# Near mirrored blocks of layer 0's first convolution through HBM, and a new order of work

## The chip, the cores and the metric

The kernel runs on one core of a Trainium2 chip. A core has a matrix engine (TensorE, PE in the profile, with its weight loads listed apart as PEld), a vector engine (VectorE, DVE), a scalar engine (ScalarE, ACT), a general engine (GpSimd, POOL) and a sync engine (SyncE, SP) that here only issues DMAs. Matmuls read SBUF and write PSUM, which has eight banks of 512 float32 columns. The metric is the device time of the whole program in microseconds: the median of 3 runs before is 2375.07 us (2373.53 to 2380.12).

## What is computed

Sixteen graphs (B = 16) of 1,024 nodes with 128 features each, in float32, go through four graph layers, each behind a layer norm and a ReLU and added to its input. All layers use the same dense 1024 x 1024 adjacency `adj` of the graph. Only layer 0 is touched by the change in what it computes where:

```python
def _adapt_conv(h, edge_weight, W, b, is_last):
    h = h @ W + b
    norm = jnp.linalg.norm(h, axis=-1, keepdims=True)
    nh = h / jnp.maximum(norm, EPS)
    cos = jnp.einsum('bij,bkj->bik', nh, nh)
    ew = edge_weight * cos
    h = jnp.einsum('bpq,bqc->bpc', ew, h)
    if not is_last:
        h = jax.nn.relu(h)
    return h
```

Layer 0 applies this three times in a row, with `edge_weight = adj`. The product `cos` (1024 x 1024) is symmetric. Layer 1 sums over neighbours and applies two linear maps, layer 2 is an attention with tanh scores, and layer 3 is an attention whose scores `e + e^T` are symmetric as well.

## The kernel before, in words

**Blocks.** A graph is cut into 8 x 8 blocks of 128 nodes. A row of blocks of the square matrix (`cos` or the scores) is made in two halves of four blocks (`HALVES`), each in one PSUM bank. So row j, half s is one bank of 128 x 512.

**The class `Square`** (from line 1387) makes such a symmetric matrix with half of the multiplications. In `row(j, s)` TensorE multiplies only the blocks on and above the diagonal (line 1415). Blocks below it are mirrored copies of blocks made before. For the near ones, those whose row and column lie in the same half, `keep` lets ACT copy the blocks to the right of the diagonal from PSUM to the SBUF tile `near` (line 1450), and `row` lets TensorE turn them (a transpose through the identity matrix) into the bank of the later row (line 1425). There are six near blocks in each half: one turn for row 1, two for row 2, three for row 3, and the same for rows 5, 6 and 7 in the second half.

The far blocks, with row in 0 to 3 and column in 4 to 7, go another way in graphs 1 to 13, where `far` holds: VectorE transposes each 32 x 32 square of them in place on its way from PSUM to the tile `quart` (line 1437), and `send` writes this to a buffer in HBM (line 1459) and fetches it with four DMAs (line 1469) so that every square stands where it belongs in the tile `got`. Rows 4 to 7 then read their first half from `got` in SBUF.

**What reads a row.** In `layer0`, one VectorE instruction per row and half (line 1645) multiplies the bank (or `got`) with the row's `1/norm` and the adjacency, `ew = cos * rn * adjT`, over 512 columns. Then `accumulate` (line 1478, convolutions 0 and 1) or `accumulate_nodes` (line 1489, convolution 2) multiplies `ew` with `h` on TensorE and adds over the rows j = 0 to 7, in that order, in two PSUM banks `acc`. ACT evicts each bank through a ReLU to `hT`, the input of the next convolution. Convolution 0 gets its own operand `hTn` by HBM also (`squares`, lines 1189 to 1202).

**The order.** The kernel first makes a list of operations, each with an engine, a length, and the buffers that it reads and writes. `Plan.order` then picks, one after the other, the operation with the smallest due time whose inputs are issued and whose buffers have a free slot. A due time is the graph's number times `PERIOD` (144.24) plus an entry of the table `TIMES`, which has one number per kind of operation; other entries hold for the first and last two graphs. `KINDS` says how many buffers of each kind may be in use at once, and how many by graphs younger than the oldest unfinished one. The result is a fixed order of instructions on every engine and on SP's queue. Up to three graphs are in work at a time, so that TensorE does one graph's sums while another waits for VectorE or for memory.

Three lines by which an operation gets its place:

```python
due = TIMES[o.key + o.edge if o.key + o.edge in TIMES else o.key][o.nth]
o.rank = (o.batch * PERIOD + due, o.seq)
...
o = next((o for o in sorted(ready, key=lambda o: (o.rank, o.seq)) if fits(o)), None)
```

Of the kernel before, what the change touches and what calls it, by code (L numbers as in the profile page):

```python
# [12 lines left out]
ALU = mybir.AluOpType  # L13
AX = mybir.AxisListType

P = 128
N = 1024
NB = N // P
D = 128
# [195 lines left out]
def tile_adj_preln(  # L215
# [40 lines left out]
    FLAGS = set("CabcdkxhyzTGmrHWMD3n")  # L256
# [62 lines left out]
    for load_it in first:  # L319
# [13 lines left out]
        "adjT": ("big", 17, 16), "adjL": ("big", 14, 4), "x": ("big", 7, 3), "w4": ("big", 21, 24),  # L333
        "chunk": ("big", 9, 8), "near": ("near", 2, 1), "quart": ("big", 5, 8), "got": ("got", 1, 1),
        "ps": ("bank", 8, 6), "acc": ("bank", 7, 6), "small": ("small", 13, 26), "row": ("row", 3, 2),
        "hbm": ("hbm", 3, 2), "hrow": ("hrow", 1, 1), "mask": ("mask", 5, 5), "dot": ("dot", 8, 5),
# [4 lines left out]
        "T DMA raw <0": [-19.5, -30.5, -48.25, -41.6, -61.6, -75.05, -5.6, -8.8],  # L341
        "T PE raw <0": [-17.1, -16.8, -16.3, -16.25, -14.25, -15.95, -19.95, -10.65, -19.15, -14.9, -15.05,
            -34.8, -5.6, 13.9, -0.2, 26.3],
        "T ACT adjT <0": [-54.3, -17.2, -22.5, -25.2, -23.65, -17.05, -24.1, -19.25, -8.5, -3.25, 4.25, 4.65,
            7.05, 1.25, -5.95, 27],
        "T DVE su <0": [50.4],
        "x DMA x <0": [-19.55, -75.2],
        "0 DVE st <0": [-46.85, -22.65],
        "0 DVE mv <0": [-18.35],
        "0 POOL rstd <0": [-31.25],  # L350
        "0 DVE nb <0": [-31.8],
        "0 DVE hn <0": [-31.8],
        "0 ACT hn <0": [-53.5],
        "0 PE ps <0": [-17.05, -17.9],
        "0 ACT hT <0": [-58.3, -37.9],
        "00 PE psP <0": [-16.35, -46.85],
        "00 DVE h <0": [-30.8, -18.25],
        "00 PE ps <0": [-33.85, -20.2],
        "00 ACT hTn <0": [-18.95, -21.35],
        "00 ACT sq <0": [-19, -23.4],  # L360
        "00 DVE ss <0": [-16.75, -16.8, -15.5],
        "00 POOL rn <0": [-24.55],
        "00 PE sq <0": [-19.9, -12.6, -12.45, -23.35, -13.9, -17.15, -8.6, -23.65, -6.3, -5.4, -38.1, 3.85,
            -34.5, -17.15, 15.35, 2.15, -3.3, -5.6, 22.9, 15.35, 1.1, 29.25],
        "00 ACT near <0": [-23.6, -53.35, -7.5, -3.35, 2.15, 24.6],
        "00 DVE ew <0": [-41.35, -7.5, -29.95, -20.25, -14.55, -0.65, 3.15, 0.8, -0.5, 1.6, 7.15, 1.05, 0.25,
            18.4, 17.3, 1.05],
        "00 ACT quart <0": [-39.85, -19.2, -39.85, -3.6],
        "00 PE acc0 <0": [-6.35, -3.35, 17, 1.55, -1.85, 3.85, -4.1, 13.8, 18.1, 1.4, 20.4, 26.75, 21.8,
            32.5, 14.05, 24.35],  # L370
        "00 POOL params <0": [-0.75, 4.8, 1.4, 36.45, 20.4, 18.95, 14.6],
        "00 DMA params <0": [-27.4],
        "00 DVE params <0": [35.2, 37.7, 35.2, 70.35, 70.35],
        "00 PE params <0": [37.2, 38.35, 72.05],
        "00 ACT hT <0": [24.55, 43.65],
        "01 PE psP <0": [-1.55, -9.25],
        "01 DVE h <0": [42.8, 43.4],
        "01 PE ps <0": [44.3, 45.8],
        "01 ACT hTn <0": [41.8, 46.55],
        "01 ACT sq <0": [41.15, 38.65],  # L380
        "01 DVE ss <0": [48.2, 39.8, 40.2],
        "01 POOL rn <0": [53.15],
        "01 PE sq <0": [34.45, 47.75, 46.1, 57, 52.35, 40.35, 52.25, 50.05, 54.5, 49.75, 41.9, 57.15, 57.2,
            64.65, 65.45, 54.45, 64.9, 60.05, 68.45, 52.85, 66.35, 69.95],
        "01 ACT near <0": [35.25, 59.5, 43.5, 58.85, 59.1, 70.95],
        "01 DVE ew <0": [48.6, 66.5, 53.65, 57.7, 55.3, 52, 54.9, 68.65, 59.8, 61.85, 64.3, 68.9, 59.95,
            62.75, 61, 70.2],
        "01 ACT quart <0": [57.15, 51.8, 54.55, 57.4],
        "01 PE acc0 <0": [58.35, 37, 54.6, 70.2, 59.45, 65.6, 61.85, 60.35, 53.2, 50.4, 66.45, 72, 67.9,
            71.05, 50.3, 71.5],  # L390
        "01 ACT hT <0": [70.5, 73.15],
        "02 PE psP <0": [52.25, 74.2],
        "02 DVE h <0": [72.55, 70.5],
        "02 PE ps <0": [71.8, 77.3],
        "02 ACT hTn <0": [73.95, 80.25],
        "02 ACT sq <0": [76.7, 65.9],
        "02 DVE ss <0": [70.8, 78.05, 79.3],
        "02 POOL rn <0": [87],
        "02 PE sq <0": [80.2, 82.35, 81.65, 87.15, 80.95, 84.05, 85.05, 84.5, 84.55, 88.8, 86.4, 91.3, 91.8,
            66.75, 84.9, 96.75, 97.3, 85.75, 97.75, 100.9, 89.3, 100.3],  # L400
        "02 ACT near <0": [72.1, 93.55, 83.8, 82.75, 71.8, 89.3],
        "02 DVE ew <0": [82.1, 82.95, 84, 78.95, 95.8, 90.3, 96.05, 79.35, 95.45, 100.65, 95.8, 101.2, 75.7,
            93.05, 78.9, 91.5],
        "02 ACT quart <0": [81.4, 83.35, 87.15, 91.85],
        "02 PE acc0 <0": [82.65, 91.55, 87.95, 91.5, 91.25, 93.75, 100.15, 84.35, 100.2, 101.85, 102.45,
            105.25, 100.65, 103.05, 94.15, 106.85],
        "02 DVE x <0": [89.85, 114.75],
        "T DMA adjT <1": [-129.75, -221.3, -169.05, -212.7, -210.4, -169.1, -204.2, -217.15],
        "T DVE adjT <1": [-141.7, -138.05, -140.15, -129.95, -122, -117.65, -114.8, -114.6],
        "T ACT su <1": [-139.85, -107.05, -109.9, -104.85, -100.25, -112.55, -110.1, -95.2],  # L410
        "1 DVE st <0": [111.95, 111.5],
        "1 DVE mv <0": [93.85],
        "1 POOL rstd <0": [107.65],
        "1 DVE nb <0": [113.9],
        "1 DVE hn <0": [109.1],
        "1 ACT hn <0": [125.3, 117.65],
        "1 DVE x <0": [136.7, 134.95, 139.35],
        "1 DMA adjL <0": [59.95, 59.15, -24.85, 49.85, 132.5, 134.85, 93.65, 118.95],
        "1 DVE adjL <0": [101.65, 57, 134.6, 108.15, 119, 123.05, 130.95, 129],
        "1 PE acc1 <0": [114, 110.25, 123.5, 127.2, 124.8, 134.45, 122.45, 123.85, 123.7, 124.75, 127.6,  # L420
            126.65, 127.45, 131.6, 129.15, 127.8],
        "1 ACT g <0": [126.8, 128.05],
        "1 PE py <0": [131.8, 131.75, 131.75, 132.05],
        "1 ACT y1 <0": [132.55, 131.6, 137.7, 134.1],
        "1 PE py2 <0": [132.3, 132.15],
        "2 DVE st <0": [139.4, 128.85],
        "2 DVE mv <0": [118.75],
        "2 POOL rstd <0": [138.9],
        "2 DVE nb <0": [142.45],
        "2 DVE hn <0": [142.4],  # L430
        "2 ACT hn <0": [132.9, 129.85],
        "2 PE ps <0": [144.25, 144.15],
        "2 ACT hnT <0": [124.6, 93.2],
        "2 DVE alone <0": [138.85],
        "2 DVE x <0": [156.9, 185.75, 183.1],
        "2 PE psP <0": [148.65, 144.15, 144.2],
        "2 ACT h <0": [142.95, 139.4, 153.85],
        "2 DVE hrow <0": [149.7],
        "2 PE pf <0": [155.7],
        "2 ACT hfl <0": [159.45],  # L440
        "2 PE pt <0": [155.75],
        "2 ACT sr <0": [148.4],
        "2 DMA sd <0": [159.85],
        "2 DMA s1 <0": [158.25],
        "2 DVE h <0": [156.95],
        "2 ACT e2 <0": [144.55, 145.45, 145.3, 155.55, 143.05, 167.15, 163.25, 167.2, 167.25, 167.9, 164.45,
            167.9, 173.55, 175.1, 167.95, 166.3],
        "2 DVE e2 <0": [162.25, 163.05, 164.8, 164.75, 86.05, 81.75, 77.9, 77.85, 172.25, 165.85, 167.4,
            166.25, 158.75, 158.65, 172.65, 178.9],
        "2 PE acc2 <0": [158.05, 166.7, 147.55, 165.8, 163.25, 150.1, 172.65, 168.45, 164.6, 157.9, 168.9,  # L450
            170.85, 141.9, 167.65, 160.85, 177.65, 175.4, 171.65, 175.2, 177.5, 175.5, 172.1, 170.25, 149.5],
        "2 DVE rden <0": [185.75, 134.75, 134.1, 183.15],
        "3 DVE st <0": [186.45, 168.3],
        "3 DVE mv <0": [184.4],
        "3 POOL rstd <0": [186.7],
        "3 DVE nb <0": [168.2],
        "3 DVE hn <0": [171.55],
        "3 ACT hn <0": [183.55, 252.45],
        "3 PE ps <0": [197.3, 190.45, 194.1, 157.05],
        "3 ACT hnT <0": [183.65, 182.3],  # L460
        "3 PE pg <0": [197.3, 196.2],
        "3 ACT gT <0": [192.7, 203],
# [1118 lines left out]
    def layer0(b, xt, aT, prepared):  # L1581
# [8 lines left out]
        for i in range(3):  # L1590
# [46 lines left out]
            for j in range(NB):  # L1637
                ew = chunk(f"ew_{k}_{j}")
                for s, (lo, hi) in enumerate(HALVES):
                    pc, view = square.row(j, s)  # L1640
                    if "k" in FLAGS:
                        square.keep(j, s, pc)
# [556 lines left out]
```

## Time and profile before

The profiled execution took 2375.19 us, of which 2373.4 are the span from the first to the last instruction.

| | us | share of the span |
|---|---|---|
| TensorE busy | 2343.0 | 99% |
| VectorE busy | 2036.7 | 86% |
| ScalarE busy | 1445.6 | 61% |
| GpSimd busy | 253.4 | 11% |
| 16 DMA engines, queue 1 | | 59.8% |

The groups around the change, with how often they occur, their busy time and the mean of one:

| line | what | count | busy us | mean ns |
|---|---|---|---|---|
| 1425 | TensorE turns, sq from near | 768 | 147.0 | 273 |
| 1425 | TensorE turns, sq from quart | 192 | 28.0 | 273 |
| 1450 | ACT copies, near from sq, three shapes | 384 | 140.0 | 367 |
| 1437 | VectorE transposes, quart from sq, 512 columns | 208 | 143.5 | 699 |
| 1645 | VectorE products, ew from sq, 512 columns | 612 | 432.4 | 738 |
| 1645 | VectorE products, ew from got, 512 columns | 156 | 112.9 | 752 |

The busy time of a group counts overlapping instructions once; the mean is the length of one instruction from start to end. Instructions of an engine overlap in part, so that the distance from start to start, which is what an engine really spends on one, is read from the timeline and not from the mean. The granted TensorE clock was 0.997 over the span.

### The profile page before, as it was taken

What the parts mean: (1) busy time and instruction counts of PE and PEld (TensorE: products, weight loads), DVE (VectorE), ACT (ScalarE), POOL (GpSimd) and SP (SyncE); (2) the same over time, 40 slices, a digit from 0 to 9 for tenths busy, and PEclk for the clock granted to TensorE, in tenths of its full rate; (3) what the DMA queues carried; (4) which work ended last, traced back from release to release, by engine and by line L of the source; (5) the groups of instructions that cost most, each with busy time, mean ns of one, the idle gap of its engine ahead of it and who ended that gap; (6) DMA issues with size and microseconds to landing.
All of it is one profiled execution on the core that took longest, in us unless ns stands there. A gap on an engine that the chain in (4) does not pass through costs nothing.

```text
span 2373.4 us, 35020 instructions
## 1 busy us (share of the span) xinstructions
PE 2343.0 (99%) x11577; PEld 1551.8 (65%) x11577; DVE 2036.7 (86%) x5570; ACT 1445.6 (61%) x2561; POOL 253.4 (11%) x168
## 2 busy tenths in 40 slices
PE   8999999999999999999999999999999999999997
PEld 5568566675757657576675766757566575765764
DVE  6658899998989989898998989989899898887777
ACT  5416764747567565666656667565666657656375
POOL 3000010101101100010101101101010100100012
PEclk9999999999999999999999999999999999999999
DMA  9135649486594957939587594856949577272200
GB/s 198 60 106 116 125 116 191 121 159 143 146 175 134 185 107 164 183 98 198 117 164 153 135 185 127 170 122 164 176 115 188 115 155 146 63 123 64 72 1 18
DMA packets 997253, 314.30 MB, mean 132 GB/s; under 512 B 682456, under 2 KB 978528, under 8 KB 997072
## 3 DMA queue, kind: packets, MB, share of 16 engines
q1 hardware_dynamic: 976912, 301.35, 59.8%
q10 hardware_dynamic: 19264, 9.70, 1.4%
q8 instruction: 92, 1.51, 0.3%
q0 software_dynamic: 896, 1.01, 0.2%
q14 instruction: 89, 0.73, 0.1%
HBM read 227.50 MB, written 84.47 MB: 131 GB/s over the span
## 4 chain that ended last, share of the span: by engine, by line
PE 95%; DVE 3%; DMA 1%; ACT 1%; SPq 0%; issue 0%; POOL 0%; ACTq 0%; DVEq 0%
PE acc L1478 36%; PE sq L1415 20%; PE acc L1489 19%; PE psP L1249 6%; PE sq L1425 4%; PE py L1713 2%; PE py L1259 2%; PE ps_hTn L1178 1%; PE pg L1259 1%; PE psN L1249 1%; DVE e L1957 1%; DVE e L1916 1%; PE ps_hnT L1178 1%; PE ps_h3T L1178 1%; DMA x<-in_x_dram 1%; DVE e L1825 0%
## 5 line engine op out<-in xcount | busy, mean ns | idle before, releaser
L1645 DVE SCALAR_TENSOR_TENSOR ew<-sq,rn,adjT 128x512 f32<-128x512 f32 x612 | 432.4, 738 | 69.8 <-PE sq L1425 40.7
L1478 PE MATMUL acc<-ew,h 128*128 128x512 f32 x1024 | 476.6, 593 | 0.3 <-DVE ew L1645 0.3
L1415 PE MATMUL sq<-hTn 128*128 128x512 f32 (+3 forms) x1152 | 430.2, 487 | 0.4 <-ACT hTn L1271 0.4
L1450 ACT COPY near<-sq 128x128 f32<-128x128 f32 (+2 forms) x384 | 140.0, 367 | 325.5 <-PE sq L1425 256.3
L1478 PEld LDWEIGHTS acc<-ew,h 128*128 128x128 f32 x1024 | 181.5, 190 | 164.8 <-issue 134.5
L1415 PEld LDWEIGHTS sq<-hTn 128*128 128x128 f32 x1152 | 193.9, 191 | 129.9 <-issue 92.5
L1489 PEld LDWEIGHTS acc<-h,ew 128*128 128x128 f32 x2048 | 244.6, 192 | 33.4 <-issue 30.1
L1489 PEld LDWEIGHTS acc<-h,e 128*128 128x128 f32 x2048 | 236.6, 192 | 21.9 <-issue 16.8
L1489 PE MATMUL acc<-h,ew 128*128 128x128 f32 x2048 | 250.3, 275 | 0.0
L1478 PE MATMUL acc<-e,hs 128*128 128x512 f32 x512 | 240.4, 597 | 2.8 <-DVE top L1937 1.5
L1489 PE MATMUL acc<-h,e 128*128 128x129 f32 x2048 | 238.1, 275 | 0.8 <-DVE e L1825 0.8
L1478 PE MATMUL acc<-adjL,hn 128*128 128x512 f32 x512 | 231.9, 596 | 2.0 <-DVE adjL L1696 2.0
L1171 POOL TENSOR_TENSOR rstd<-ve,mhalf 128x8 f32<-128x8 f32 x64 | 105.2, 1644 | 787.3 <-DVE ve L1330 769.9
L1916 DVE CUSTOM_DVE_ANT_0 e<-mask,sq 128x512 f32<-128x512 int8 x204 | 136.1, 680 | 48.3 <-ACT near L1450 46.3
L1825 DVE SCALAR_TENSOR_TENSOR e<-adjT,e 128x512 f32<-128x512 f32 x256 | 162.7, 684 | 12.4 <-ACT e L1821 12.0
L1948 ACT ACTIVATE e<-e,top 128x1024 f32<-128x1024 f32 x128 | 146.6, 1146 | 41.4 <-DVE top L1937 40.0
L1957 DVE TENSOR_TENSOR e<-e,adjT 128x512 f32<-128x512 f32 x248 | 169.1, 701 | 2.5 <-ACT e L1948 2.5
L1171 POOL TENSOR_TENSOR rn<-ss,mhalf 128x8 f32<-128x8 f32 x48 | 83.3, 1736 | 817.3 <-DVE ss L1632 700.1
L1478 PEld LDWEIGHTS acc<-adjL,hn 128*128 128x128 f32 x512 | 95.6, 191 | 112.2 <-issue 102.6
L1425 PEld LDWEIGHTS sq<-ident,near 128*128 128x128 f32 x768 | 101.4, 141 | 81.8 <-issue 56.0
L1478 PEld LDWEIGHTS acc<-e,hs 128*128 128x128 f32 x512 | 91.4, 192 | 95.2 <-issue 72.5
L1817 ACT ACTIVATE e<-s,h 128x1024 f32<-128x1024 f32 x128 | 143.8, 1139 | 13.4 <-DMA s<-sd 13.4
(167 smaller groups left out, 3782.0 us busy)
## 6 DMA issues: line engine op xcount, KB each, us to landing
adjL<-in_adj_dram SPq DMA_DIRECT2D x128, 512.0 KB
adjT<-in_adj_dram SPq DMA_DIRECT2D x480, 128.0 KB
by_hbm<-quart SPq DMA_DIRECT2D x104, 512.0 KB
got<-by_hbm SPq DMA_DIRECT2D x416, 128.0 KB
s<-sd SPq DMA_DIRECT2D x15, 512.0 KB
out_dram<-z ACTq DMA_DIRECT2D x15, 512.0 KB
d_hT<-hn SPq DMA_DIRECT2D x14, 512.0 KB
hT<-d_hT SPq DMA_DIRECT2D x56, 128.0 KB
```

Of the source, the lines that this page charges most:

```text
L1171: pool_op(1.64, [src], [dst], lambda: nc.gpsimd.tensor_tensor(dst.t, src.t, mhalf, op=ALU.pow))
L1249: nc.tensor.matmul(dst.t[:, (c - lo) * n : (c - lo + 1) * n], one(srcT, c), w, start=True, stop=True)
L1415: lambda: nc.tensor.matmul(dst.t[:, (first - lo) * P :], one(leftT, j), some(rightT, first, hi), start=True, stop=True),
L1425: nc.tensor.transpose(cols(dst.t, r), cols(kept.t, p), ident)
L1478: lambda s=s, lo=lo, hi=hi: nc.tensor.matmul(acc[s].t, cols(h.t, at, w), span(ew.t, lo, hi), start=(j == 0), stop=(j == NB - 1)),
L1489: nc.tensor.matmul(a.t[:, (c - lo) * n : (c - lo + 1) * n], cols(ew.t, c), h.t[:, at * w : at * w + n], start=(j == 0 and c == lo), stop=( ...
L1645: lambda view=view, ew=ew, rn=rn, j=j, lo=lo, hi=hi: nc.vector.scalar_tensor_tensor(like(view(), span(ew.t, lo, hi)), view(), rn.t[:, j : ...
L1817: lambda e=e, j=j: nc.scalar.activation(e.t[:, 0:N], s1.t[:, 0:N], AF.Tanh, bias=h.t[:, j * E2 + D + 1 : j * E2 + D + 2]),
L1825: lambda e=e, j=j, lo=lo, hi=hi: nc.vector.scalar_tensor_tensor(span(e.t, lo, hi), span(aT[j].t, lo, hi), 0.0, span(e.t, lo, hi), op0=ALU. ...
L1916: lambda e=e, view=view, mask=mask, peak=peak, s=s, lo=lo, hi=hi: nc.vector.tensor_tensor_reduce(like(view(), span(e.t, lo, hi)), like(vie ...
L1948: lambda e=e, top=top, tot=tot: nc.scalar.activation(e.t[:, 0:N], e.t[:, 0:N], AF.Exp, bias=top.t, accum_out=tot.t),
L1957: lambda e=e, j=j, lo=lo, hi=hi: nc.vector.tensor_mul(span(e.t, lo, hi), span(e.t, lo, hi), span(aT[j].t, lo, hi)),
```

## The change

A second flag in the class `Square`, `near_too`, is set for convolution 0 of layer 0 in graphs 2 to 13 (`far(b, 0)` and `b > 1`; of the letters "ABV" only "A" is among the flags; for layer 3 the letter "X" is absent). There, the near blocks are mirrored like the far ones: VectorE transposes their 32 x 32 squares from PSUM to one of two tiles `laid`, a store puts them in HBM, and four fetches per half bring them to a tile `back`. TensorE turns none of them, and ACT copies none. The rows that have mirrored near blocks are read in two pieces, one from PSUM and one from `back`. All entries of `TIMES` are new, and so are most of `KINDS`.

```diff
-    FLAGS = set("CabcdkxhyzTGmrHWMD3n")
+    FLAGS = set("CabcdkxhyzTGmrHWMD3nA")
...
-        "adjT": ("big", 17, 16), "adjL": ("big", 14, 4), "x": ("big", 7, 3), "w4": ("big", 21, 24),
-        "chunk": ("big", 9, 8), "near": ("near", 2, 1), "quart": ("big", 5, 8), "got": ("got", 1, 1),
-        "ps": ("bank", 8, 6), "acc": ("bank", 7, 6), "small": ("small", 13, 26), "row": ("row", 3, 2),
-        "hbm": ("hbm", 3, 2), "hrow": ("hrow", 1, 1), "mask": ("mask", 5, 5), "dot": ("dot", 8, 5),
+        "adjT": ("big", 16, 16), "adjL": ("big", 13, 5), "x": ("big", 5, 3), "w4": ("big", 23, 33),
+        "chunk": ("big", 11, 11), "near": ("near", 2, 1), "quart": ("big", 6, 6), "back": ("big", 7, 1),
+        "got": ("got", 1, 1), "ps": ("bank", 8, 8), "acc": ("bank", 7, 4), "small": ("small", 28, 22),
+        "row": ("row", 4, 5), "hbm": ("hbm", 2, 3), "hrow": ("hrow", 2, 2), "mask": ("mask", 5, 5),
+        "dot": ("dot", 7, 7),
...
+        "00 DMA near": [-46.5, -23.3],
+        "00 DMA back": [-64.45, -19.05],
...
-        "00 ACT hT": [-37.35, -17.2],
+        "00 ACT hT": [-24.35, -11.7],
...
+            if near_too:
+                self.laid = [Buf("near", [P, 6 * P], f"laid_{k}_{s}") for s in range(2)]
+                self.back = [Buf("back", [P, N], f"back_{k}_{s}") for s in range(2)]
+            else:
+                self.near = Buf("near", [P, 6 * P], f"near_{k}")
...
+            if self.near_too and lo < j < hi:
+                back, (c, x, y) = self.back[s], self.MIRRORED[n]
+
+                def shares():
+                    return back.t[:, 0 : 6 * P].rearrange("p (x c i) -> p c x i", c=2, i=SQ)[:, c, x:y]
+
+                return [(dst, lambda: by_block(dst.t[:, n * P :], D, 4 - n), j, hi), (back, shares, lo, j)]
...
+        MIRRORED = {1: (0, 8, 12), 2: (0, 0, 8), 3: (1, 0, 12)}
+        LAID = {0: ((1, 1, 2, 0), (2, 2, 0, 0)), 1: ((2, 2, 1, 0),), 2: ((3, 1, 2, 1),)}
...
+            if self.near_too and lo <= j and first < hi:
+                laid = self.laid[s]
+                for q, n, x, c in self.LAID[j - lo]:
+                    dve(
+                        V(n * P) + 0.04, [blk(read, q, q + n)], [(laid, (j - lo) * P, (j - lo + 1) * P)],
+                        lambda q=q, n=n, x=x, c=c: nc.vector.transpose(
+                            laid.t.rearrange("p (h x c i) -> p h x c i", x=3, c=2, i=SQ)[:, :, x, c : c + n],
+                            read.t[:, q * P : (q + n) * P].rearrange("p (q h i) -> p h q i", h=P // SQ, i=SQ),
+                        ),
+                    )
+                if j - lo == 2:
+                    self.send_near(s)
+                return
...
+        def pieces(self, j, s):
+
+            if (j, s) not in self.known:
+                for j2 in range(j, j + QUARTER) if self.near_too else (j,):
+                    for s2 in (0, 1) if self.near_too else (s,):
+                        self.known[j2, s2] = self.row(j2, s2)
+                        self.keep(j2, s2, self.known[j2, s2][0][0])
+            return self.known.pop((j, s))
+
+        def send_near(self, s):
+
+            laid, back = self.laid[s], self.back[s]
+            by_hbm = Buf("hbm", [N, D], f"near_hbm_{self.k}_{s}")
+
+            def rows():
+                return by_hbm.t[0 : 6 * P].rearrange("a f -> (a f)")
+
+            op(
+                "DMA", 0.7, [laid], [by_hbm],
+                lambda: nc.sync.dma_start(
+                    rows().rearrange("(h p e) -> p h e", p=P, e=6 * SQ),
+                    laid.t.rearrange("p (h e) -> p h e", e=6 * SQ),
+                ),
+                lat=2.2,
+            )
+
+            def squares_to_places():
+                src = rows().rearrange("(h g a x e) -> h a x g e", h=P // SQ, g=P // SQ, a=SQ, e=2 * SQ)
+                for h in range(P // SQ):
+                    nc.sync.dma_start(
+                        back.t[h * SQ : (h + 1) * SQ, 0 : 6 * P].rearrange("p (x g e) -> p x g e", g=P // SQ, e=2 * SQ), src[h]
+                    )
+
+            op("DMA", 1.5, [by_hbm], [back], squares_to_places, lat=2.4)
...
-            square = Square(k, hTn, hTn, "abc"[i] in FLAGS and far(b, i))
+            square = Square(k, hTn, hTn, "abc"[i] in FLAGS and far(b, i), "ABV"[i] in FLAGS and far(b, i) and b > 1)
...
-                    pc, view = square.row(j, s)
-                    if "k" in FLAGS:
-                        square.keep(j, s, pc)
-                    o = dve(
-                        V(HALF, True), [pc, rn, blk(aT[j], lo, hi)], [blk(ew, lo, hi)],
...
+                    pieces = square.pieces(j, s)
+                    for pc, view, lo, hi in pieces:
+                        o = dve(
+                            V((hi - lo) * P, True), [pc, rn, blk(aT[j], lo, hi)], [blk(ew, lo, hi)],
...
```

Layer 3 reads its squares by the same `pieces`; without the letter "X" it gets one piece per row and half, as before.

## The prediction

> **What bounds the kernel now.** I read the page's busy shares first, then the table of stretches for the same shares by place, then the chain of waits for the price of a turn.
>
> ```profile
> PE 2343.0 (99%) x11577; PEld 1551.8 (65%) x11577; DVE 2036.7 (86%) x5570; ACT 1445.6 (61%) x2561; POOL 253.4 (11%) x168
> PE 95%; DVE 3%; DMA 1%; ACT 1%; SPq 0%; issue 0%; POOL 0%; ACTq 0%; DVEq 0%
> 0.00:144.00 144.00, 135.16 (x659) 89.55 (x660) 94.20 (x219) 64.87 (x136) 28.28 (x41) 1.00 0.59 121
> ...
> 1008.00:1152.00 144.00, 144.00 (x708) 95.16 (x707) 129.78 (x356) 90.07 (x157) 13.74 (x8) 1.00 0.73 150
> ...
> 2304.00:2448.00 144.00, 55.31 (x261) 34.62 (x260) 54.16 (x161) 40.60 (x79) 18.56 (x8) 0.96 0.02 8
> ```
>
> The last three lines are stretches of 144 us: busy time of PE, PEld, DVE, ACT and POOL, then granted TensorE clock, DMA share and GB/s. In the middle PE is busy 144.00 of 144: TensorE never waits there, and the clock is full. Of the 30.4 us in which PE is idle (2373.4 - 2343.0), 8.8 lie in the first stretch and 14.1 in the last (2373.4 - 2304 = 69.4, less 55.31). DVE is the nearest other engine: 129.78 of 144.
>
> ```profile
> 1000.85 1.79 PE psN L1249 x16
> ...
> 1033.49 0.33 PE sq L1425 x3
> ...
> 1144.00 1.79 PE psN L1249 x16
> ```
>
> These are steps of the chain of waits (start, length, what). The same 16 matmuls recur after 143.15 us: that is the period of one graph, and it is all TensorE work. Line 1425 is the turn that the change removes: three of them hold the chain 0.33 us, so one costs 0.11 us.
>
> **What goes from TensorE.** A convolution turns six near blocks in each half of its columns, 12 in all. In 12 graphs (2 to 13) that makes 144 turns at 0.11 us: 15.8 us, all on the chain. The group's mean for one turn is 273 ns, but [...]turns overlap. Here a rule matters: the Trainium skill, "TensorE: Matmul & The Clock Gate", Part 4 (PE-mode transpose), gives about 275 ns for a transpose in a kernel's context. The trace agrees with that duration (273); by it the gain would be 144 x 0.275 = 39.6 us. But successive starts are 0.11 apart, so I take 15.8. The turns' weight loads are hidden under other matmuls (PEld 65%) and give nothing.
>
> **What comes onto VectorE.** Eight transposes from PSUM per graph, four of one block and four of two, and six products more, because rows 1 to 3 and 5 to 7 are now taken in two pieces. The nearest rows, from DVE's timeline (start, length, what):
>
> ```profile
> 1032.25 0.71 DVE L1437 STREAM_TRANSPOSE quart<-sq 128x512 f32<-128x512 f32 x1
> 1032.88 1.37 DVE L1645 SCALAR_TENSOR_TENSOR ew<-sq,rn,adjT 128x512 f32<-128x512 f32 x2
> ...
> 1056.83 2.19 DVE L1293 SCALAR_TENSOR_TENSOR x<-o,rden,x 128x128 f32<-128x128 f32 x8
> ```
>
> A transpose of 512 columns is followed by the next operation after 0.63 us. Eight products of 128 columns take 2.19 us and one alone 0.35, so each further one adds 0.263; three of 512 columns in another row take 2.06 with 0.74 for one alone, so 0.66. The line through 0.263 and 0.66 has 0.00103 us per column and 0.13 us fixed. One block then costs 0.26 and two 0.40: 4 x 0.26 + 4 x 0.40 = 2.64 us. Six further instructions cost 6 x 0.13 = 0.8. The sum is 3.4 us per graph. DVE has 129.78 x 143.15/144 = 129.0 us per graph now; it would have 132.4 of a period of 143.15 - 12 x 0.11 = 141.83, or 93%, with 9.4 us free where it had 14.1. I take the 3.4 as hidden behind TensorE; uncovered, it would cost 3.4 x 12 = 41 us.
>
> ACT loses six copies a graph, (0.263 + 0.370 + 0.469) x 2 = 2.2 us by the group means of the three shapes; it is busy 90 of 144 and this is worth nothing.
>
> **The trip through memory, and the SP queue.** Per half there is one store and four fetches of a quarter each. The far blocks of the same convolution take this way now (rows of the timelines of SP and of DVE: start, length, engine, line):
>
> ```profile
> 1140.43 0.39 SPq L1459 DMA_DIRECT2D by_hbm<-quart  x1
> ...
> 1144.02 1.78 SPq L1469 DMA_DIRECT2D got<-by_hbm  x4
> ...
> 1153.54 2.04 DVE L1645 SCALAR_TENSOR_TENSOR ew<-got,rn,adjT 128x512 f32<-128x512 f32 x3
> ...
> 1083.61 1.24 DVE L1202 STREAM_TRANSPOSE hTn<-hTn 128x1024 f32<-128x1024 f32 x1
> ```
>
> From the store's issue to the fetch's is 3.6 us, and four fetches take 1.8 to issue. When they land is seen where VectorE waited for such fetches (of hTn, hnT and hT): 2.0, 2.6 and 4.5 us after the last issue. So a trip is some 8 us (7.4 to 9.9). Is it on a path? In this graph the operand hTn is ready at 1084.9, the squares run from 1104.65 (row 0) to 1161.1 (row 7), and the output's first half is evicted at 1161.1: TensorE does other graphs' work for most of 56 us. First half: row 2's blocks leave at 1124.3 and a trip would end before 1134, while row 3 itself comes at 1136.4; the far parts come behind it anyway. Second half: rows 4 to 7 are made at 1155 to 1161, at the last moment, which a trip of 8 us forbids. They must be made some 10 us earlier, which hTn allows by 20 us and PSUM by its banks; the new table has the second store due 11.6 us before the second eviction (-23.3 and -11.7), for a trip of 8, three products (1.2 us) and a last sum (0.86). Cost taken: nothing. Bounds: nothing, if rows 4 to 6 come early enough; 8 x 12 = 96 us, if TensorE stood through every second trip. The nearest row is the far trip, which TensorE sits out without a wait, so I take nothing; but this one is tight.
>
> On SP every issue counts: 2 x (0.39 + 1.78 + the wait of 3.2 for the store) = 10.7 us per graph, and what is queued behind a waiting fetch (loads of adjL and adjT, the next far store) stands that long. The longest SP wait on its list is 48.5 us, with TensorE still full, so 10.7 us are covered. The traffic: per half 384 KB each way, 512 pieces of 768 B out and 1,536 of 256 B in, so 24 x 2,048 = 49,152 packets on 997,253, or 5%. At queue 1's mean (59.8% of 16 engines for 976,912 packets, 23 ns a packet) this is 5.9 us of all 16 engines per graph, raising the DMA share from 0.73 to 0.77.
>
> A rule speaks against the change: "VectorE: DVE Perf Modes", section Rules for kernel authors, says to turn a 128x128 block on TensorE where a PSUM destination will do. In latency it is right: 0.11 us against 0.26 on VectorE and a trip of 8. Priced by its table of transpose paths (390 ns against 311), swapping would gain 0.08 us a block if one engine did both, some 11 us. Here the engines differ: full TensorE loses 0.11, and VectorE has room. I follow the rows.
>
> **The order searched anew, and the buffer limits.** All due times change, and the shares of buffers with them (more rows of the square in flight, one adjT buffer fewer). In the middle there is nothing to win or lose while PE stays full. At the two ends there are 30.4 us of idle time; a different order may move them either way. Nearest row: the head's 8.8 includes a 7.2 us wait for the first load, which no order removes, and the last graphs' tail is a chain through DVE. I take nothing, with 6 us either way.
>
> **Sum.** The profiled execution ran 2375.19 us (span 2373.4 and 1.8 around it), 0.12 above the median of 2375.07. 2375.2 - 15.8 = 2359.4 us; against the median 2359.3. Its own range is 2353 to 2366.
>
> **Rivals.** (1) VectorE becomes a local bound. For: DVE is busy 11.97 of 12 us in 1008 to 1020 even now, and goes to 93% on average. Against: it is full there and PE does not wait. If a quarter of the 3.4 us stands open, 0.85 per graph, the change gains 15.8 - 10.2 = 5.6: 2369.6 us. It would break even at 1.32 of the 3.4 us.
> (2) Slower: TensorE stands before the second half's last sums (rows 5 to 7) because the second trip has not landed. For: 8 + 1.2 + 0.9 = 10.1 of the 11.6 us are spoken for, and DMA shares over 1.0 of the 16 engines show in 1080 to 1116. Against: due times set an order, not times, and other sums can stand in front. It decides from 1.32 us of wait per graph; with 3 us, (3 - 1.32) x 12 = 20 more: 2395 us.
> (3) The search also finds a better head or tail, a third of the 30.4 us: 2359.4 - 10.1 = 2349.3 us. For: 14.1 us stand idle in the last stretch. Against: the tail is VectorE's there.
> That the change does not do what it says is unlikely: the new flag is read for the first convolution alone.
>
> **How the numbers follow.** Forecast 0.66, (1) 0.13, (2) 0.13, (3) 0.08. The range takes nearly all of the forecast, most of (1) and half of (3): 2350 to 2373. Within 0.3% (2367.9 to 2382.2) is what a measurement here cannot tell from no change. Faster: the forecast, (3) and somewhat under half of (1), 0.80. Same: the rest of (1), 0.08. Slower: (2), 0.12 without its edge.
>
> **What would show it.** Right: 624 near turns left in line 1425's group instead of 768, the period at 141.8 us, PE still 144.00 of 144 in the middle, DVE near 133. Wrong: TensorE idle before accumulations with VectorE's product as releaser (rival 1), or with the fetch behind that product (rival 2), or an unchanged period.

## The result, and the profile after

The changed kernel takes 2363.03 us (median of 6, 2361.8 to 2364.85) beside 2373.48 us of the kernel before in the same series (median of 6). The ratio of the two is 0.9952 with a 95% interval of 0.9939 to 0.9965; it is not taken from the medians, whose quotient is 0.9956. So the change gains 10.4 us by the medians and 11.4 by the ratio; 2359 was forecast, with a range of 2350 to 2373. Its profiled execution ran 2363.82 us, with a span of 2360.7, 12.7 us less than the 2373.4 of before.

First the page's busy shares and its chain of waits by engine, then the table by stretches (columns as before). Most of the new 2% of SPq in the chain are DMA issues in the first 60 us:

```profile
PE 2327.0 (99%) x11433; PEld 1536.6 (65%) x11433; DVE 2069.4 (88%) x5738; ACT 1427.9 (60%) x2489; POOL 251.6 (11%) x168
...
PE 92%; DVE 3%; SPq 2%; DMA 1%; ACT 1%; issue 0%; POOL 0%; ACTq 0%; DVEq 0%
```

```profile
0.00:144.00 144.00, 134.24 (x658) 88.28 (x659) 94.37 (x220) 65.51 (x136) 27.65 (x41) 1.00 0.63 135
...
1008.00:1152.00 144.00, 144.00 (x697) 94.45 (x696) 133.24 (x371) 90.11 (x153) 14.68 (x9) 1.00 0.76 161
...
2304.00:2448.00 144.00, 39.72 (x156) 21.96 (x154) 41.46 (x125) 32.01 (x64) 12.98 (x6) 0.94 0.02 8
```

TensorE has 144 instructions fewer (11,577 less 11,433) and is busy 16.0 us less. In the middle it is still full, 144.00 of 144. But it is idle for 33.7 us in all (2360.7 - 2327.0) where it was idle for 30.4. Those 3.3 us are the difference between the 16.0 and the 12.7. To find their place, one follows a mark that both kernels pass: the 16 projection matmuls (output psN) at the end of a graph's layer 3. First the kernel before, then the changed one, both from TensorE's timeline (start, length):

```profile
1143.83 1.95 PE L1249 MATMUL psN<-eye,hpT 128*128 128x131 f32 x16
1286.98 1.95 PE L1249 MATMUL psN<-eye,hpT 128*128 128x131 f32 x16
...
2148.08 1.95 PE L1249 MATMUL psN<-eye,hpT 128*128 128x131 f32 x16
2321.06 2.04 PE L1249 MATMUL psN<-eye,hpT 128*128 128x131 f32 x16
2360.68 2.05 PE L1249 MATMUL psN<-eye,hpT 128*128 128x131 f32 x16
```

```profile
1133.80 1.95 PE L1251 MATMUL psN<-eye,hpT 128*128 128x131 f32 x16
1275.63 1.95 PE L1251 MATMUL psN<-eye,hpT 128*128 128x131 f32 x16
...
2132.11 1.95 PE L1251 MATMUL psN<-eye,hpT 128*128 128x131 f32 x16
2305.50 2.24 PE L1251 MATMUL psN<-eye,hpT 128*128 128x131 f32 x16
2346.34 2.05 PE L1251 MATMUL psN<-eye,hpT 128*128 128x131 f32 x16
```

The period fell from 143.15 to 141.83 us, by 1.32; in 12 graphs that is 15.8 us. At the third mark from the end the changed kernel is 15.97 us ahead, as much as the turns give. At the last mark it is 14.34 ahead and at the end of the span 12.7. So the last two graphs give back 3.3 us, 1.2 of them in the last graph's layer 3 (39.62 against 40.84 between the last two marks) and 1.6 after it (12.72 against 14.36 to the end).

### The profile page after: what moved, and what is told of

The parts are those of the page before. It is cut to its first block, busy times and chain, and to the rows that moved or that the text cites. A ratio compares the mean times of both kernels' runs of the same rounds, so it can differ in the third digit from the quotient of the medians.

```text
span 2360.7 us, 35122 instructions
## 1 busy us (share of the span) xinstructions
PE 2327.0 (99%) x11433; PEld 1536.6 (65%) x11433; DVE 2069.4 (88%) x5738; ACT 1427.9 (60%) x2489; POOL 251.6 (11%) x168
## 4 chain that ended last, share of the span: by engine, by line
PE 92%; DVE 3%; SPq 2%; DMA 1%; ACT 1%; issue 0%; POOL 0%; ACTq 0%; DVEq 0%
PE acc L1543 34%; PE sq L1422 20%; PE acc L1554 19%; PE psP L1251 6%; PE sq L1439 3%; PE py L1774 2%; PE py L1261 2%; SPq L1630 2%; PE ps_hTn L1180 1%; PE pg L1261 1%; PE psN L1251 1%; PE ps_hnT L1180 1%; DVE e L1978 1%; DVE e L2007 1%; PE ps_h3T L1180 1%; SPq L1606 1%
## 5 line engine op out<-in xcount | busy, mean ns | idle before, releaser
L1543 PE MATMUL acc<-ew,h 128*128 128x512 f32 x1024 | 465.9, 593 | 0.5 <-DVE ew L1709 0.5
L1709 DVE SCALAR_TENSOR_TENSOR ew<-sq,rn,adjT 128x512 f32<-128x512 f32 (+3 forms) x612 | 409.0, 703 | 37.9 <-PE sq L1439 13.9
L1422 PE MATMUL sq<-hTn 128*128 128x512 f32 (+3 forms) x1152 | 424.0, 487 | 1.5 <-DVE peak L1978 0.7
L1480 ACT COPY near<-sq 128x384 f32<-128x384 f32 (+2 forms) x312 | 113.6, 369 | 322.9 <-PE sq L1439 275.8
L1554 PEld LDWEIGHTS acc<-h,e 128*128 128x128 f32 x2048 | 234.8, 192 | 15.2 <-issue 10.5
L1638 DVE STREAM_TRANSPOSE adjT<-adjT 128x1024 f32<-128x1024 f32 x120 | 147.8, 1233 | 2.7 <-DMA adjT<-in_adj_dram 2.7
L1422 PE MATMUL sq<-h3T,gT 128*128 128x512 f32 (+3 forms) x384 | 144.2, 488 | 1.8 <-DVE peak L1978 0.8
```

Source lines behind the costliest of these rows:

```text
L1422: lambda: nc.tensor.matmul(dst.t[:, (first - lo) * P :], one(leftT, j), some(rightT, first, hi), start=True, stop=True),
L1480: lambda: nc.scalar.copy(span(kept.t, p, p + hi - first), read.t[:, (first - lo) * P :]),
L1543: lambda s=s, lo=lo, hi=hi: nc.tensor.matmul(acc[s].t, cols(h.t, at, w), span(ew.t, lo, hi), start=(j == 0), stop=(j == NB - 1)),
L1554: nc.tensor.matmul(a.t[:, (c - lo) * n : (c - lo + 1) * n], cols(ew.t, c), h.t[:, at * w : at * w + n], start=(j == 0 and c == lo), stop=( ...
L1638: dve(V(N), [t], [t], lambda t=t: nc.vector.transpose(t.t, t.t), True)
L1709: lambda view=view, ew=ew, rn=rn, j=j, lo=lo, hi=hi: nc.vector.scalar_tensor_tensor(like(view(), span(ew.t, lo, hi)), view(), rn.t[:, j : ...
```

## Experiments

### The changed kernel once more

No edit. Each series of runs has the kernel before in it; this run belongs to the same series as laid_x2, queue_stands and turns_back_tail below, in which the kernel before had a median of 2374.75 us.

> The changed kernel unaltered, on the chip and beside the runs that follow. Every theory: 2363, ratio 0.995 to the kernel before.

Measured: 2362.84 us, ratio 0.9949 (0.9935 to 0.9963), as in the first series.

### The turns put back as filler

Run turns_back. `made` is what TensorE now does for one row and half of the square: the matmul as before, then n turns, the count that was there before the change.

```diff
+                def made(n=min(hi, j) - lo if self.near_too else 0):
...
+                    for r in range(n):
+                        nc.tensor.transpose(cols(dst.t, r), one(leftT, j), ident)
```

> The changed kernel with 144 turns put back as filler: in the first convolution of graphs 2 to 13 TensorE turns a block of its own operand into the columns of the bank that nothing reads, one, two or three times per row, just where the mirrored blocks were turned before. All else stays: the trip through memory, VectorE's transposes and pieces, the order of work. Theory 1 (a full TensorE: the turns and nothing else made the gain, at 0.11 us each): 15.8 us more than the changed kernel's 2363.0, so 2379, and a graph's period of 143.14 us instead of 141.83. If a turn cost its full length of 0.273 us: 39 us more, 2402. Theory 2 (VectorE was the limit of part of the gain): less than 12 us more, since TensorE would have waited in those places anyway.

Measured: 2376.88 us, ratio 1.0013 to the kernel before (1.0006 to 1.0019). That is 13.9 us above the changed kernel by the medians, 14.5 by the two ratios and 15.2 by the spans of the two profiled executions. Theory 1 had said 15.8, Theory 2 less than 12. The period decides:

```profile
1141.95 1.95 PE L1251 MATMUL psN<-eye,hpT 128*128 128x131 f32 x16
1285.10 1.95 PE L1251 MATMUL psN<-eye,hpT 128*128 128x131 f32 x16
```

These marks of TensorE's timeline are 143.15 us apart: with the turns, the old period is back to the hundredth. A turn on a full TensorE is worth 0.11 us, and the 273 ns of its record are not what it costs. The run also isolates the rest: the trip, VectorE's work and the new order, without the saving, cost 0.13% (0.06 to 0.19), some 3 us.

### One due time in the tail

Run tail_issue. In the last graph the output leaves in two halves, and ACT does the tanh as well as the sends. ACT's timeline of the changed kernel (in brackets the idle time before, and what ended it):

```profile
2352.01 0.72 ACT L2089 ACTIVATE z<-z,half 128x512 f32<-128x512 f32 x1
2354.28 0.38 ACTq L2127 DMA_DIRECT2D out_dram<-z  x1
2354.71 0.63 ACT L2088 ACTIVATE z<-z 128x512 f32<-128x512 f32 x1 [1.98 <-DVE z L2102]
```

The send of the first half (ACTq) stands in front of the second half's tanh. It must wait for VectorE's last product of that half, and the tanh, whose input was ready earlier, waits behind it. In the kernel before, both sends stood behind the tanh; there ACT's timeline ends with them:

```profile
2368.03 0.72 ACT L2039 ACTIVATE z<-z,half 128x512 f32<-128x512 f32 x1
2368.42 1.98 ACTq L2077 DMA_DIRECT2D out_dram<-z  x2
```

The order was planned with DMAs as an engine of their own, so the planner does not see that a send holds ACT.

```diff
-        "3 DMA z >0": [202.55, 228.45],
+        "3 DMA z >0": [228.4, 228.45],
```

> One due time: the first half of the last graph's output is sent after the second half's two tanh on ACT's queue and not before them, as in the kernel before. In the changed kernel ACT stands 1.98 us before that tanh, behind the send, which waits for VectorE. Theory 1 (part of the missing gain lies in the order of the last graph): 1.6 us less than the changed kernel, 2361.4, the stretch from the last projections to the end 12.7 us instead of 14.4. If the tail is set elsewhere (the last load or VectorE): no difference.

Measured: 2360.43 us, ratio 0.9943 (0.993 to 0.9955), span 2359.3. ACT's timeline of this run:

```profile
2353.25 0.63 ACT L2088 ACTIVATE z<-z 128x512 f32<-128x512 f32 x1 [0.45 <-DVE z L2102]
2353.91 0.72 ACT L2089 ACTIVATE z<-z,half 128x512 f32<-128x512 f32 x1
2354.30 1.97 ACTq L2127 DMA_DIRECT2D out_dram<-z  x2
```

The wait fell from 1.98 to 0.45 us, and the stretch from the last mark (2346.41) to the end is 12.9 us instead of 14.36. All five executions (2360.07 to 2361.2) lie below all ten of the changed kernel in the other two series. The median fell by more than the 1.5 us of the stretch, by 2.6 (1.4 to 2.1 by the ratios). Some 0.4 of the rest has a visible place: between the last two marks the granted clock was 1.00 in this execution and 0.96 in the changed kernel's, and they are 40.40 instead of 40.84 us apart. What remains lies within the intervals of the ratios. This is the fastest version of the study.

### Both at once

Run turns_back_tail: the edits of the two runs above together.

> The turns put back, and the send of the last graph's first half moved behind the tanh, both at once. Turns put back alone came out 0.13% above the kernel before (about 3 us), which is all that the change costs apart from the turns. If 1.5 to 2.5 us of these 3 are the misplaced send: 0.02 to 0.06% above the kernel before, 2374.5 to 2375.5 beside 2373.8. If the send is not the cause: 0.13% again.

Measured: 2375.7 us, ratio 1.0007 (0.9998 to 1.0015). That cannot be told from the kernel before, but the interval holds the 0.02 to 0.06% expected with the send as the cause and the 0.13% expected without it, so this run alone doesn't decide. By the traces of the two single runs the send is about half of the 3 us. The largest other part is the 1.2 us of the last graph's layer 3, for which the timeline has a likely cause (last section), but which was not tried.

### More work for VectorE

Run laid_x4; laid_x2, further down, is the same edit with `range(2)`.

```diff
-                        lambda q=q, n=n, x=x, c=c: nc.vector.transpose(
+                        lambda q=q, n=n, x=x, c=c: [nc.vector.transpose(
...
-                        ),
+                        ) for _ in range(4)],
```

> Every transpose of the near blocks on VectorE is made four times over, which adds 3 x 2.64 = 7.9 us of VectorE time to a graph: from 131.5 busy (133.5 of 144, taken to the period) to 139.4 of 141.83 us, 98%. Theory 1 (VectorE's share of the change is covered and has room): within 4 us of 2363.0, TensorE still 144.00 of 144 in the middle. Theory 2 (VectorE is already a local limit and ate part of the gain): at least half of the added time shows, 12 x 4 = 48 us more, 2411, with TensorE idle behind VectorE's products.

Measured: 2426.53 us, ratio 1.0222 (1.0207 to 1.0238), 63 us above the changed kernel.

```profile
1008.00:1152.00 144.00, 141.41 (x683) 91.64 (x682) 137.61 (x383) 87.29 (x149) 13.70 (x8) 1.00 0.74 159
```

In this stretch TensorE is full no longer (141.41 of 144), and VectorE, at 137.61, isn't either. The list of waits names the first as waiting for the second (us in total, times, longest):

```profile
PE acc L1543 <- DVE ew L1709: 20.0, 22, 1.0
PE acc L1543 <- DVE e L2007: 8.3, 22, 0.7
```

Six periods between two marks (1168.75 and 2051.60) give 147.14 us, 5.3 more than 141.83. The edit delays the store of the near blocks too, and SP's queue behind it. But VectorE's waits for what SP fetches hardly change (8.2 us for `back` beside 7.1 in the changed kernel, 1.7 for `adjT` beside 2.7), so it is VectorE's time that is short. By the number Theory 2 is met. The added time, however, is more than the 7.9 us of the expectation, as VectorE's timeline of this run shows:

```profile
1135.53 1.33 DVE L1468 STREAM_TRANSPOSE laid<-sq 128x128 f32<-128x128 f32 x4
1136.78 1.07 DVE L1349 TENSOR_SCALAR hn<-x,mv,rstd 128x128 f32<-128x128 f32 x4
...
1139.83 1.89 DVE L1468 STREAM_TRANSPOSE laid<-sq 128x256 f32<-128x256 f32 x4
1141.64 0.25 DVE L1757 TENSOR_TENSOR adjL<-adjL,ident_e 128x128 f32<-128x128 f32 x1
```

Four transposes of one block hold VectorE for 1.25 us and four of two blocks for 1.81, where in the changed kernel one takes 0.22 and 0.36 from its start to the next operation's. Over the graph that is 10 us more, not 7.9. So 10 us of work made 5.3 us of loss. A smaller dose tells whether the first part was free. It was expected before that reading, with 2.64 us for the dose; by the same reading it is 3.3 us:

> The near transposes on VectorE made twice instead of four times: 2.64 us more of VectorE time for a graph. With four times, 7.9 us more lengthened the period by 5.1 us. Theory A (VectorE has a fixed room of 7.9 - 5.1 = 2.8 us per graph before TensorE waits): within 3 us of the changed kernel, period 141.83 to 142.1. Theory B (what VectorE gets more shows from the start, in proportion, 64%): 1.7 us per graph, 20 us more, 2383.

Measured: 2365.68 us, ratio 0.9962 (0.9949 to 0.9976), 2.8 us above the 2362.84 of the changed kernel in the same series; of its nine stretches from 576 to 1872 us all but one have 144.00, that one 143.87. Eight periods between marks (708.48 and 1845.14) give 142.08 us, 0.25 more. Both lie just inside what Theory A allowed and far from Theory B. So VectorE took in 3.0 of the first 3.3 us, and 4.7 of 10: its room is some 3 to 5 us per graph, and no sharp limit. It is idle for 10.3 us of the changed kernel's period (141.83 less 133.5 x 141.83/144 = 131.5). More than half of that idle time lies where added transposes can't use it in this order.

### A longer trip

Run trip_longer.

```diff
-                src = rows().rearrange("(h g a x e) -> h a x g e", h=P // SQ, g=P // SQ, a=SQ, e=2 * SQ)
+                extra = hbm.tile([N, D], F32, tag=f"extra_{s}", name=f"extra_{self.k}_{s}")
+                nc.sync.dma_start(extra[0 : 6 * P], by_hbm.t[0 : 6 * P])
+                src = extra[0 : 6 * P].rearrange("a f -> (a f)").rearrange("(h g a x e) -> h a x g e", h=P // SQ, g=P // SQ, a=SQ, e=2 * SQ)
```

> Each of the 24 trips of the near blocks takes one more leg, a copy from HBM to HBM of the same 384 KB between the store and the fetches, in the same place of SP's queue: 3 to 5 us longer than the 7.4 us it takes now. Theory 1 (the trip is covered): within 3 us of 2363.0. Theory 3 (the second trip is tight, as 10.1 of 11.6 us in the due times made me fear): from 1.5 us on each graph pays, 12 x (4 - 1.5) = 30 us more, 2393, with TensorE waiting before the first convolution's last sums.

Measured: 2422.84 us, ratio 1.0209 (1.0195 to 1.0223), 60 us above the changed kernel, twice what Theory 3 gave. VectorE's wait for the fetched near blocks, from the list of waits, first in the changed kernel, then here (us in total, times, longest):

```profile
DVE ew L1709 <- DMA back<-near_hbm: 7.1, 10, 2.5
```

```profile
DVE ew L1711 <- DMA back<-extra: 75.9, 24, 6.2
```

In the changed kernel 10 of the 24 trips come late for VectorE, by 0.7 us on average, and TensorE hides it. With the longer trip all 24 do. While VectorE stands before a product nothing behind it gets through, of any graph, and TensorE soon stands too, mostly at another place: the largest PE wait of this run is for another layer's `hn` (28.0 us in 12 waits), which is queued behind that product. Here is one of them, from the timelines of VectorE and of TensorE, and below them TensorE's next 4 us (busy time, granted clock, DMA share, GB/s):

```profile
1186.24 0.88 DVE L1711 SCALAR_TENSOR_TENSOR ew<-back,rn,adjT 128x384 f32<-128x384 f32 x2 [4.69 <-DMA back<-extra]
1187.04 1.11 DVE L1349 TENSOR_SCALAR hn<-x,mv,rstd 128x128 f32<-128x128 f32 x4
```

```profile
1187.44 1.24 PE L1180 MATMUL ps_hnT<-ident,hn 128*128 128x128 f32 x4 [3.02 <-DVE hn L1349]
```

```profile
1187.44:1191.44 4.00, 4.00 (x9) 0.59 0.00 0
```

The period is 147.09 us, by two marks of the same graphs (1164.69 and 2047.21). The wait is not the whole loss: after it the granted clock was 0.59 for 4 us. The same holds after ten of the eleven such waits from 452 us on (0.57 to 0.63); in the changed kernel's steady part no stretch of 2 us is below 0.97. Summed over stretches of 2 us, the missing share of the clock comes to an estimated 19 us of the 60, the tail left out. Theory 3 had counted the late time alone.

### Only the queue stands

The longer trip makes SP stand 3 us longer as well, before its later loads. Run queue_stands has that without late data:

```diff
+                extra = [hbm.tile([N, D], F32, tag=f"extra_{s}_{i}", name=f"extra_{self.k}_{s}_{i}") for i in (0, 1)]
+                nc.sync.dma_start(extra[0][0 : 6 * P], by_hbm.t[0 : 6 * P])
+                nc.sync.dma_start(extra[1][0:SQ], extra[0][0:SQ])
```

> Where the longer trip cost 60 us, two things changed at once: the near blocks came 3 us later, and SP's queue stood 3 us longer. Here only the queue stands: behind the four fetches SP issues the same copy from HBM to HBM and then a small one that waits for it; the near blocks are fetched as early as in the changed kernel. If the late data made the loss (VectorE in order behind a product that waits): within 4 us of the changed kernel, VectorE's waits for the fetched blocks near the 7.1 us they have now. If the standing queue made it (late loads of adjT, adjL and the far blocks): most of the 60 us again.

Measured: 2382.07 us, ratio 1.0029 (1.0018 to 1.0041), 19 us above the changed kernel of the same series. Neither expectation is met. VectorE's waits for `back` are 8.9 us, near the 7.1, but a new one has come (from the list of waits of this run):

```profile
DVE adjT L1641 <- DMA adjT<-in_adj_dram: 30.3, 26, 3.6
```

In the changed kernel this wait is 2.7 us, in 2 times. So the standing queue makes about a third of the loss without late near blocks, through adjacency tiles that arrive late; the rest of the 60 us needs the late near blocks. The added copies also carry 9.8 MB beside the 320.2 of queue 1, and this run doesn't part that traffic from the standing. How the two losses add up when both are there is not settled: with the longer trip, no wait for `adjT` is among VectorE's large ones, since VectorE stands elsewhere already.

## Why the prediction was right, and where it was off

**The bound and the turns: right.** The signs that were named came: 624 near turns are left, TensorE is full in the middle (144.00 of 144), VectorE is at 133.2 there, and a graph's period fell to 141.83 us, as worked out. The price of 0.11 us from the step in the chain held, and the 0.273 of the record's length would have been off by a factor of 2.5. (The "latency" of 0.11 us that the prediction sets against VectorE's 0.26 is this step too; a turn's length is 0.273.)

**VectorE's share: right in sign, and no part of the steady gain was lost to it.** It came to 131.5 - 129.0 = 2.5 us per graph against 3.4. The transposes were oversized: in DVE's timeline one of a block is followed after 0.22 us and one of two blocks after 0.36, not 0.26 and 0.40. But the statement that 9.4 us would be free was wrong in its meaning: the idle time is 10.3 us, and of added transposes only some 3 to 5 us found room in it. Rival 1 did not come about, but stood nearer than the idle time suggested.

**The trip: right that it costs nothing, for a weaker reason than given.** The estimate of 8 us holds: the second trip of one graph, from the store's issue at 1143.28 on SP to its first product on VectorE at 1150.70, took 7.4. "This one is tight" was right, and the tightness is VectorE's: 10 of 24 trips are awaited there. Rival 2 named TensorE's last sums as the place; the longer trip showed VectorE's queue, where a late block holds all graphs.

**The SP queue: the argument failed.** "The longest SP wait on its list is 48.5 us, with TensorE still full, so 10.7 us are covered" does not follow. A long wait in one place of a queue says nothing of the cover in another, and 3 us more in two places per graph, with the copies that made them, cost 19 us. The 10.7 us were in fact covered (TensorE is full in the middle), in an order searched for them; the argument given does not carry that, so here the right answer was luck. So was the sum: issuing four near fetches takes 2.6 us and not 1.8, but the wait for the store is 2.5 and not 3.2.

**The ends: the term that was mis-sized.** "I take nothing, with 6 us either way" stood for the new order at head and tail. It measured +3.3 us in the last two graphs. About half of it is a send in front of a tanh on ACT's queue, shown by moving it; 1.2 us have only a likely cause. In the head the new order won 0.8 us (at the third mark, 571.26 before and 566.49 after, it is 4.77 ahead, where the three graphs' turns give 3.96), and lost it again before the third mark from the end.

**The number was closer than the account.** The sum started from the profiled execution of 2375.19 us. The median of before in the series of the result is 2373.48; from there the sum is 2357.7, and 2363.0 misses it by 5.3 us, not by 3.7. The tail accounts for 3.3 of them. The rest has no place in the traces; single executions of the kernel before lie anywhere between 2371 and 2380 us.

## What to carry to other kernels

Where one engine is full in the steady part, as here, the saving is the count times the step from start to start, and it can be read to the hundredth from a mark that recurs once per period. Idle time of another engine is not cover: add work in doses and measure each dose in the trace, because here 10 us more cost 5.3 although 10.3 were idle. A wait in an in-order queue is passed on to everything behind it, and a wait that reaches TensorE can cost more than itself, since the granted clock may be low after it. After any new order, look at the last few microseconds separately, and at DMA issues that stand in front of compute on the same queue.

## What the runs showed of the hardware

In these traces a VectorE operation takes three times its length beside one of GpSimd. VectorE's and GpSimd's timelines of the changed kernel's last graph:

```profile
2323.76 0.69 DVE L1956 TENSOR_SCALAR mask<-adjT 128x1024 int8<-128x1024 f32 x1
...
2330.89 2.40 DVE L1956 TENSOR_SCALAR mask<-adjT 128x1024 int8<-128x1024 f32 x1
...
2333.82 2.22 DVE L2007 TENSOR_TENSOR e<-e,adjT 128x512 f32<-128x512 f32 x1
```

```profile
2330.35 2.39 POOL L2095 TENSOR_TENSOR z<-z,gate 128x1024 f32<-128x1024 f32 x1 [8.48 <-ACT z L2089]
2332.82 2.67 POOL L2096 TENSOR_TENSOR z<-z,x 128x1024 f32<-128x1024 f32 x1
```

The same mask takes 0.69 us alone and 2.40 when GpSimd starts just before it; it ends 0.55 us after GpSimd's operation. The product `e` with two inputs in SBUF takes 2.22 instead of 0.67. The Trainium skill, "SBUF — State Buffer", section Who interferes with whom, describes an exclusive lock on a port pair that VectorE and GpSimd share, held for a whole instruction, which fits these rows. It is a likely cause of the 1.2 us in the last graph's layer 3. By the excess over 0.69 and 0.67 per instruction, three stretched rows lost 4.8 us there, where those of the kernel before lost 3.7. The clock is not the cause: the last two marks are 39.62 us apart in the kernel before and 40.8 to 40.9 in the five executions with the new order that have the same granted clock between them (0.96); in the four with 1.00 they are 40.4 to 40.5 apart. But there is only one trace of the kernel before, and no run here took the collision away.
